# The last expert block of a mixture-of-experts layer: its rows reach their tokens by a product with a gate matrix instead of through memory

## The chip, the cores and the metric

One core of a Trainium2 chip runs the whole program. The metric is the device time of one execution in microseconds (us). A profiled execution is one further run with the hardware profiler on; it has its own time, and a span from its first to its last instruction.

## The reference

The program computes two layers of a small image network on x of shape (4, 384, 32, 32): four images of 1024 tokens with 384 channels. The first layer is attention with relative-position tables and a feed-forward net; the second is a sum of depthwise convolutions and a mixture of four experts. The change concerns only the last part, the experts (S = 1024 tokens of each of B = 4 images, top 2 of 4 experts, hidden size 1536):

```python
def _L1_ffn_ref(x, gate_w, gate_b, w1, b1, w2, b2):
    ...
    topk_vals, topk_idx = jax.lax.top_k(probs, TOP_K)
    mask = jnp.sum(jax.nn.one_hot(topk_idx, NUM_EXPERTS, dtype=probs.dtype), axis=-2)
    masked = probs * mask
    masked = masked / (jnp.sum(masked, axis=-1, keepdims=True) + 1e-09)
    h = jax.nn.gelu(jnp.einsum('bsd,edh->ebsh', x, w1) + b1[:, None, None, :], approximate=False)
    y = jnp.einsum('ebsh,ehd->ebsd', h, w2) + b2[:, None, None, :]
    out = jnp.einsum('bse,ebsd->bsd', masked, y)
    return out
...
t = t + _L1_ffn_ref(_ln_t(t), L1_ffn_gate_w, L1_ffn_gate_b, L1_ffn_w1, L1_ffn_b1, L1_ffn_w2, L1_ffn_b2)
```

A token's output is thus its input plus the outputs of its two experts, each times a gate. All data is float32.

## The kernel before

The kernel computes only the two chosen experts of each token. Tokens are sorted by expert into a buffer in device memory, xs_d, and the experts work through it in **blocks** of 128 rows. As four experts may each leave a block partly filled, there are ALL = 67 blocks. They are cut into four groups, one for each image that becomes ready; the last group has 22 (k = 0 to 21). Results go block by block into y_d, also in device memory, and each token picks its two rows out of it.

`blocks(g, more)` runs a group. `fetch` gathers a block's 128 token rows (xg) with an indirect DMA issued on GpSimd (POOL). `weights` gathers half an expert's weights (w, 2.5 MB) in the same way, `turn` transposes the rows on TensorE (PE) into xT. Then come twelve steps ff: three products into e_ps, a gelu on ScalarE (ACT) into eh, and two steps later, in `second`, the product y_ps. After the last of these VectorE (DVE) adds the bias into yo, and SyncE (SP) writes yo to y_d. So a block's yo is made when PE is already two steps into the next block; only the last block has none behind it.

`more(g, k)` is called after each step and lets other work take its turn in the program's order: the layers ahead, and in the last group from block NOT_LAST = 6 on, `combine(range(B - 1))`. Up to that block all rows of images 0 to 2 are in y_d. `result_rows` computes on DVE the row numbers (row, and as integers pos) of every token of an image. Then twelve times, for 256 tokens at once, `results` gathers four times 128 rows out of y_d on POOL (the tile rows, 16 buffers, always two steps ahead), `weigh` scales the first of each pair on ACT and adds the scaled second on DVE, and `finish` transposes the sums on PE into out_ps, adds them on DVE to the tokens, and lets SP write them out. Tiles out_ps have the PSUM tag m, which has two buffers; e_ps has the tag h (three buffers) and y_ps the tag y (two).

For the last image, image 3, the same is done after all blocks, with `combine([B - 1])`: 16 gathers, all issued ahead of its first `weigh`, and four times `weigh` and `finish`. Its tokens are still on chip, in the tile xb. The source of these gathers is all of y_d:

```python
y_rows = y_d if end else y_d[: (groups[-1]["start"] + NOT_LAST) * BLK]
...
for _ in groups[-1]["combined"]:
    pass
for _ in combine([B - 1]):
    pass
```

The order of instructions on each engine is made by a scheduler from the program's order and the data dependencies between tiles, unless an instruction is wrapped in `pin`, which keeps it in program order. Waits follow from the same dependencies. Every engine then executes its own list in order.

The tile img holds the zero-padded image (128 partitions x 3 x 38 x 38) that the convolutions of an image read. After the convolution of image 3 nothing uses it.

Of the kernel before, what the change touches and what calls it, by code (L numbers as in the profile page):

```python
# [11 lines left out]
F32 = mybir.dt.float32  # L12
AF = mybir.ActivationFunctionType
# [38 lines left out]

NOT_LAST = (2 * (B - 1) * N + NEXP * (BLK - 1)) // BLK - sum(COUNTS[:-1])
MAXB = B * N // BLK
OUTSIDE = 1e6


# [779 lines left out]
def result_rows(nc, small, image, pieces):  # L837


    shape = list(image["mask"].shape)  # L840

    def new(shape, name):
        return small.tile(shape, F32, tag=f"p_{name}", name=f"p_{name}", bufs=1)

    pos, part, step = new(shape, "pos"), new(shape, "prod"), new([P, 1, NEXP], "step")
    nc.vector.tensor_tensor(pos, image["rank"], bcast(pieces[0][1].unsqueeze(1), 1, shape[1]), ALU.add)
    for (_, off0), (lo, off) in zip(pieces, pieces[1:]):
        nc.vector.tensor_tensor(step[:, 0, :], off, off0, ALU.subtract)
        nc.vector.tensor_tensor(part, image["rank"], bcast(lo.unsqueeze(1), 1, shape[1]), ALU.is_ge)
        nc.vector.tensor_tensor(part, part, bcast(step, 1, shape[1]), ALU.mult)  # L850
        nc.vector.tensor_tensor(pos, pos, part, ALU.add)
    row = new([P, shape[1], 2], "fpos")
    for i, pick in enumerate(chosen(nc, new, image["mask"])):
        nc.vector.tensor_tensor(part, pick, pos, ALU.mult)
        nc.vector.tensor_reduce(row[:, :, i : i + 1], part, AX.X, ALU.add)
    nc.vector.tensor_copy(image["pos"], row)


def block_list(nc, small, cst, group, parts, done):
# [76 lines left out]
def rest_phase(tc, cst, x, ao_d, ins, xs_d, y_d, x2_d, out):  # L936
# [9 lines left out]
    with ExitStack() as es:  # L946
# [344 lines left out]
        def blocks(g, more):  # L1291

            xT, xgs = {}, {}

            def fetch(k):
                xg = ld.tile([P, C], F32, tag="xg", name="xg")
                load = nc.gpsimd.indirect_dma_start(
                    xg, None, from_xs, bass.IndirectOffsetOnAxis(ap=g["slot"][:, k, :], axis=0),
                    bounds_check=NEXP * CAP - 1, oob_is_err=False,
                )  # L1300
                for other in g["after"]:
                    after(load, other)
                xgs[k] = xg

            def turn(k):
                xg = xgs.pop(k)
                t = work.tile([P, KC, BLK], F32, tag="xT", name="xT")
                ps = ps_y.tile([P, KC, BLK], F32, tag="t", name="xT_ps")
                for c in range(KC):
                    nc.tensor.transpose(ps[:, c, :], xg[:, c * P : (c + 1) * P], ident)  # L1310
                nc.scalar.copy(t, ps)  # L1311
                xT[k] = t

            def weights(k, fh):
                w = wts[(g["start"] + k) % 2][fh]
                nc.gpsimd.indirect_dma_start(  # L1316
                    w, None, ins["w12"], bass.IndirectOffsetOnAxis(ap=g["row"][:, k, fh : fh + 1], axis=0),
                    bounds_check=NEXP * 2 * P - 1, oob_is_err=False,
                )
                return w  # L1320

            pend = []

            def second(k, ff, hs, w, py):
                o = WB + ff % FH * C
                nc.tensor.matmul(py, hs, w[:, o : o + C], start=(ff == 0), stop=(ff == NF - 1))  # L1326
                if ff == NF - 1:
                    yo = hid.tile([P, C], F32, tag="yo", name="yo", bufs=2)
                    nc.vector.tensor_tensor(yo, py, w[:, WB + FH * C :], ALU.add)  # L1329
                    n = (g["start"] + k) * BLK  # L1330
                    nc.sync.dma_start(y_d[n : n + BLK, :], yo)


            fetch(0)
            ws = {h: weights(*divmod(h, 2)) for h in range(3)}
            turn(0)
            for k in range(g["nb"]):
                py = ps_y.tile([P, C], F32, tag="y", name="y_ps", bufs=2)
                for ff in range(NF):
                    fh, f = divmod(ff, FH)  # L1340
                    h = 2 * k + fh
                    w = ws[h]
                    if ff == 0 and k + 1 < g["nb"]:
                        fetch(k + 1)
                    ph = ps_h.tile([P, BLK], F32, tag="h", name="e_ps")
                    for c in range(KC):
                        o = c * FH * P + f * P
                        nc.tensor.matmul(ph, w[:, o : o + P], xT[k][:, c, :], start=(c == 0), stop=(c == KC - 1))  # L1348
                    hs = hid.tile([P, BLK], F32, tag="eh", name="eh")
                    o = KC * FH * P + f  # L1350
                    nc.scalar.activation(hs, ph, AF.Gelu, bias=w[:, o : o + 1])  # L1351
                    pend.append((k, ff, hs, w, py))
                    if len(pend) > 2:
                        second(*pend.pop(0))
                    if f == 2 and h + 3 < 2 * g["nb"]:
                        ws[h + 3] = weights(*divmod(h + 3, 2))
                    if ff == NF // 2 and k + 1 < g["nb"]:
                        turn(k + 1)
                    more(k)
            for p in pend:  # L1360
                second(*p)

        def combine(bs):


            w = 2 * P
            end = bs[-1] == B - 1
            y_rows = y_d if end else y_d[: (groups[-1]["start"] + NOT_LAST) * BLK]
            pieces = [p for g in groups for p in g["pieces"]]

            def finish(b, n0, xr, zs):
                for c0, c1 in ((0, 2), (2, 3)):
# [7 lines left out]
            def results(b, n0):  # L1380

                zs = []
                for j in range(2):
                    ys = [new_row() for _ in range(2)]
                    for i, y in enumerate(ys):
                        index = images[b]["pos"][:, n0 // P + j, i : i + 1]
                        nc.gpsimd.indirect_dma_start(y, None, y_rows, bass.IndirectOffsetOnAxis(ap=index, axis=0))
                    zs.append(ys)
                if end:
                    return zs, xbs[b][:, :, n0 : n0 + w]  # L1390
                t0 = b * N + n0
                xr = ld.tile([P, KC, w], F32, tag="xr", name="xr")
                nc.sync.dma_start(xr, x2_d[:, t0 : t0 + w].rearrange("(k p) n -> p k n", p=P))
                return zs, xr

            def weigh(b, n0, zs):
                for j, (z, y) in enumerate(zs):
                    gate = images[b]["gate"][:, n0 // P + j, :]
                    nc.scalar.activation(z, z, AF.Copy, scale=gate[:, 0:1])
                    nc.vector.scalar_tensor_tensor(z, y, gate[:, 1:2], z, ALU.mult, ALU.add)  # L1400
                return [z for z, _ in zs]

            if not end:
                for b in (*bs, B - 1):
                    result_rows(nc, small, images[b], pieces)
                    yield 3.0, 0.0
            todo = [(b, n0) for b in bs for n0 in range(0, N, w)]
            ahead = {}
            for i, (b, n0) in enumerate(todo):
                for more in todo[i : i + (len(todo) if end else 2)]:  # L1410
                    if more not in ahead:
                        ahead[more] = results(*more)
                zs, xr = ahead[b, n0]
                for _ in range(0 if end else 5):
                    yield 0.3, 0.0
                zs = weigh(b, n0, zs)
                for _ in range(0 if end else 5):
                    yield 0.3, 0.1
                finish(b, n0, xr, zs)

        xbs, marks = {}, {}

# [91 lines left out]
        def spend(steps):  # L1514
            cost = next(steps, None)
            if cost:
                clock[0] += cost[0]
                clock[1] += cost[1]
            return cost

        def more(g, k):
            clock[0] += 0.05
            clock[1] += 1.36
            if g is groups[-1] and k == NOT_LAST and "combined" not in g:
                g["combined"] = combine(range(B - 1))
            spend(g.get("combined", iter(())))
            while clock[0] < clock[1] and spend(todo):
                pass

        for i, g in enumerate(groups):  # L1530
            blocks(g, lambda k: more(g, k))
            if i + 1 < len(groups):
                while "after" not in groups[i + 1]:
                    next(todo)
        for _ in groups[-1]["combined"]:
            pass
        for _ in combine([B - 1]):
            pass


# [108 lines left out]
```

## Time and profile before

| | |
|---|---|
| three runs | 3029.85, 3033.38, 3039.24 us (median 3033.38) |
| profiled execution | 3047.33 us, span 3045.6 us |
| mean granted PE clock | 0.981 of full speed |
| PE busy | 2916.2 us, 96% of the span |
| DVE busy | 1958.9 us, 64% |
| ACT busy | 1371.9 us, 45% |
| POOL busy | 1158.8 us, 38% |
| gathers rows<-y_d, all 64 | 957 ns each on POOL (median) |
| the last 16 of them | the first at 3016.6, the last at 3036.0 us |

A share of the span says how much an engine works over the whole program, which has several stages with different limits. For the end of the program the chain of waits is the view to read: it goes back from the last instruction to what released it, step by step. Lines in the views name the line of the kernel's text, the engine, and the tile that is written and those that are read (out<-in), without buffer numbers.

### The profile page before, as it was taken

Reading aid. Unit: us, or ns where it says so; the run is one execution under the profiler, and the core shown is the slowest. Engines: PE = TensorE matmul, PEld = TensorE weight load, DVE = VectorE, ACT = ScalarE, POOL = GpSimd, SP = SyncE. Lnnn points to the kernel's source line nnn. Section 1 sums busy time; section 2 is a strip of 40 time slices with the busy share of each in tenths; the row PEclk is TensorE's granted clock in tenths of the full one; section 3 lists DMA queues with packets and bytes.
Section 4 is the critical chain, followed back from the end, with each engine's and each line's share of the span. In section 5 each row is a group of like instructions: output and inputs, shape, how many; then the busy total and the mean of one; then the engine's idle time right before and its main releaser. Section 6 shows DMA issues by size and latency. Waiting matters only on the chain.

```text
span 3045.6 us, 63467 instructions
## 1 busy us (share of the span) xinstructions
PE 2916.2 (96%) x25391; PEld 2018.2 (66%) x25391; DVE 1958.9 (64%) x3577; ACT 1371.9 (45%) x2833; POOL 1158.8 (38%) x1121
## 2 busy tenths in 40 slices
PE   9999999999999999999899889999999999999996
PEld 4556777677777777777533347776577877777775
DVE  3237787777787877787478879999899640001101
ACT  1116766666767676666312332433342243233332
POOL 1115555565656474737300213251124232124412
PEclk9999999999999999999999889999999999999998
DMA  4447667666676766765400405724243055356742
GB/s 156 140 150 218 156 215 161 212 162 217 160 226 155 219 166 206 174 206 155 168 21 35 145 16 192 280 105 153 96 167 126 26 224 228 132 227 252 275 178 73
DMA packets 291720, 500.56 MB, mean 164 GB/s; under 512 B 135632, under 2 KB 221520, under 8 KB 283744
## 3 DMA queue, kind: packets, MB, share of 16 engines
q1 hardware_dynamic: 201760, 269.93, 28.9%
q0 software_dynamic: 37520, 201.63, 17.9%
q10 hardware_dynamic: 52144, 24.94, 4.0%
q8 instruction: 200, 3.28, 0.5%
q14 instruction: 96, 0.79, 0.1%
HBM read 543.58 MB, written 152.37 MB: 229 GB/s over the span
## 4 chain that ended last, share of the span: by engine, by line
PE 74%; DVE 14%; issue 4%; DMA 3%; ACT 2%; POOL 2%; SPq 0%; another core or an unknown queue 0%; POOLq 0%; DVEq 0%; ACTq 0%
PE e_ps L1348 13%; PE y_ps L1326 13%; DVE xb L1136 8%; PE t_ps L430 7%; PE sc_ps L249 7%; PE av_ps L249 7%; PE tabq_ps L249 6%; PE qk_ps L211 4%; PE a_ps L440 3%; PE v_ps L174 2%; PE tv_ps L249 2%; PE proj_ps L1024 2%; DMA s<-sd 1%; PE tap_ps L1184 1%; DVE extra L422 1%
## 5 line engine op out<-in xcount | busy, mean ns | idle before, releaser
L1348 PEld LDWEIGHTS e_ps<-xT,w 128*128 128x128 f32 x4824 | 654.7, 192 | 216.3 <-issue 11.7
L373 POOL TENSOR_TENSOR bias<-b,s 128x416 f32<-128x416 f32 (+24 forms) x656 | 660.7, 1044 | 185.4 <-DMA s<-sd 169.0
L1348 PE MATMUL e_ps<-xT,w 128*128 128x128 f32 x4824 | 668.9, 276 | 13.2 <-ACT xT L1311 5.7
L1326 PE MATMUL y_ps<-w,eh 128*128 128x384 f32 x1608 | 650.8, 490 | 13.1 <-ACT eh L1351 12.7
L1136 DVE SCALAR_TENSOR_TENSOR xb<-img,pack,xb 128x1024 f32<-128x1024 f32 (+1 forms) x539 | 634.5, 1242 | 0.0
L1351 ACT ACTIVATE eh<-e_ps,w 128x128 f32<-128x128 f32 x804 | 293.6, 367 | 717.4 <-PE e_ps L1348 650.6
L1316 POOL DMA_INDIRECT w<-in_w,row x134 | 174.8, 1305 | 731.9 <-PE y_ps L1326 302.7
L422 DVE TENSOR_REDUCE extra<-arow 128x32 f32<-128x32 f32 (+24 forms) x768 | 380.0, 550 | 9.0 <-ACT arow L411 5.5
L401 DVE CUSTOM_DVE_ANT_0 arow<-sc_ps,bias 128x1024 f32<-128x1024 f32 x256 | 311.7, 1218 | 104.8 <-issue 52.0
L411 ACT ACTIVATE arow<-arow,nm 128x1024 f32<-128x1024 f32 x256 | 302.2, 1180 | 68.6 <-DVE nm L401 59.3
L430 PEld LDWEIGHTS t_ps<-ident,arow 128*128 128x128 f32 x2048 | 219.8, 141 | 169.1 <-ACT aT L431 100.6
L431 ACT COPY aT<-t_ps 128x512 f32<-128x512 f32 x512 | 278.6, 604 | 92.2 <-PE t_ps L430 90.3
L430 PE MATMUL t_ps<-ident,arow 128*128 128x128 f32 x2048 | 281.3, 280 | 12.1 <-ACT arow L411 12.1
L1329 DVE TENSOR_TENSOR yo<-y_ps,w 128x384 f32<-128x384 f32 x67 | 37.1, 554 | 392.0 <-PE y_ps L1326 387.2
L249 PE MATMUL sc_ps<-kk,qs 48*32 48x512 f32 x4096 | 276.4, 602 | 6.9 <-DVE nm L401 5.7
L1326 PEld LDWEIGHTS y_ps<-w,eh 128*128 128x128 f32 x1608 | 248.2, 193 | 26.8 <-ACT eh L1351 15.7
L249 PEld LDWEIGHTS av_ps<-aT,vb 128*64 128x64 f32 x4096 | 222.3, 137 | 51.8 <-ACT aT L431 40.0
L338 DVE STREAM_TRANSPOSE b<-tabk_ps 128x480 f32<-128x480 f32 x256 | 218.7, 983 | 35.9 <-PE tabk_ps L249 35.9
L249 PE MATMUL av_ps<-aT,vb 128*64 128x128 f32 x4096 | 237.7, 274 | 0.4 <-ACT aT L431 0.4
L249 PE MATMUL tabq_ps<-tab,kq 48*128 48x480 f32 x512 | 219.5, 578 | 5.7 <-ACT st L342 3.5
L249 PE MATMUL tabk_ps<-tab,kq 48*128 48x480 f32 x512 | 222.6, 581 | 0.0
L249 PEld LDWEIGHTS tabq_ps<-tab,kq 48*128 48x128 f32 x512 | 148.5, 295 | 45.5 <-ACT aT L431 5.6
(212 smaller groups left out, 3136.3 us busy)
## 6 DMA issues: line engine op xcount, KB each, us to landing
sd<-st SPq DMA_DIRECT2D x128, 480.0 KB
s<-sd SPq DMA_DIRECT2D x256, 240.0 KB
xs_d<-arow SPq DMA_DIRECT2D x64, 384.0 KB
tvw<-in_tv SPq DMA_DIRECT2D x120, 192.0 KB
y_d<-yo SPq DMA_DIRECT2D x67, 192.0 KB
qk_d<-vb POOLq DMA_DIRECT2D x48, 256.0 KB
qs<-qk_d SPq DMA_DIRECT2D x256, 48.0 KB
kq<-qk_d ACTq DMA_DIRECT2D x56, 192.0 KB
```

The source lines that it names most:

```text
L249: ins = nc.tensor.matmul(*args, **kw)
L338: turn = nc.vector.transpose(b2.rearrange("p e y x -> p x (e y)")[:, i + j], ps[:, j, : SPAN * IMG])
L373: nc.gpsimd.tensor_tensor(bias[:, y0:y1, :], bass.AP(b2.tensor, b2.offset + (e * IMG + y0) * IMG, [list(b2.ap[0]), [(step * IMG + 1) * IMG ...
L401: nc.vector.tensor_tensor_reduce(s["flat"], ps.rearrange("p h n -> p (h n)"), s["bias"].rearrange("p y x -> p (y x)"), -SCALE, BIG, ALU.ad ...
L411: nc.scalar.activation(s["flat"], s["flat"], AF.Exp, bias=s["nm"], scale=-1.0, accum_out=dn[:, y % YT : y % YT + 1])
L422: pin(nc.vector.tensor_reduce(ex[:, i, :], a[:, p0:p1, :].rearrange("p y x -> p x y"), AX.X, ALU.add))
L430: pin(nc.tensor.transpose(pt[:, j, :], s["flat"][:, k0 : k0 + P], ident))
L431: pin(nc.scalar.copy(aT[:, 4 * g : 4 * g + 4, s["y"] % YB, :], pt))
L1136: ins_ = nc.vector.scalar_tensor_tensor(acc[:, k, y0:y1], img[:, k, dy + y0 : dy + y1, dx : dx + IMG], w7[:, k, dy, dx : dx + 1], acc[:, k ...
L1326: nc.tensor.matmul(py, hs, w[:, o : o + C], start=(ff == 0), stop=(ff == NF - 1))
L1348: nc.tensor.matmul(ph, w[:, o : o + P], xT[k][:, c, :], start=(c == 0), stop=(c == KC - 1))
L1351: nc.scalar.activation(hs, ph, AF.Gelu, bias=w[:, o : o + 1])
```

## The change

1. The last block's result (rows LAST = 66 x 128 and up of y_d) is no longer written to y_d. It stays on chip in yo.
2. `choose` builds a matrix on chip, picked, of 128 x 1024: entry (r, t) is the gate with which row r of the last block counts for token t of image 3, or zero. For each 128 tokens DVE compares the tokens' row numbers, less LAST, with a line 0 to 127 and multiplies with the gates (twice, for the two experts), adds the two, PE transposes, and ACT copies into picked. It advances by one piece with each step of `combine(range(B - 1))`.
3. picked, the line and the working tiles of `choose` lie in the memory of img.
4. The 16 gathers of image 3 read y_d[:LAST] with a bounds check. Rows beyond it aren't fetched, and their gates are set to zero in the tile e_kept. The gathers are put into the program at the first call of `more` after the next-to-last block's yo, which is in the last block.
5. After the blocks come `weigh`, as before but pinned in program order, and `close` in place of `finish`: out_ps is the product of yo and picked plus the sums times the identity matrix, all added up in PSUM. It uses one PSUM tile of each of the tags m, h and y, and DVE adds each of the three to the tokens.

```diff
+        kept = small.tile([P, nj, 2], F32, tag="e_kept", name="e_kept", bufs=1)
+        room = img.rearrange("p k y x -> p (k y x)")
+        picked, line = room[:, :N], room[:, N : N + P]
+
+        def choose(row):
+            gate = images[B - 1]["gate"]
+            rel = small.tile([P, nj, 2], F32, tag="e_rel", name="e_rel", bufs=1)
+            nc.vector.tensor_scalar_add(rel, row, -float(LAST))
+            nc.vector.tensor_scalar(kept, rel, 0.0, None, ALU.is_lt)
+            nc.vector.tensor_tensor(kept, kept, gate, ALU.mult)
+            for n0 in range(0, P, MAXB):
+                nc.vector.tensor_scalar_add(line[:, n0 : n0 + MAXB], pc["blocks"], float(n0))
+            yield
+            last = None
+            for j in range(nj + 1):
+                if last is not None:
+                    ps = ps_m.tile([P, P], F32, tag="m", name="pick_ps")
+                    nc.tensor.transpose(ps, last, ident)
+                    nc.scalar.copy(picked[:, (j - 1) * P : j * P], ps)
+                if j < nj:
+                    hits = [room[:, N + (1 + j % 2 * 2 + i) * P :][:, :P] for i in range(2)]
+                    for i, hit in enumerate(hits):
+                        nc.vector.tensor_scalar(
+                            hit, line, rel[:, j, i : i + 1], gate[:, j, i : i + 1], ALU.is_equal, ALU.mult
+                        )
+                    last, other = hits
+                    nc.vector.tensor_tensor(last, last, other, ALU.add)
+                yield
...
-            y_rows = y_d if end else y_d[: (groups[-1]["start"] + NOT_LAST) * BLK]
+            y_rows = y_d[:LAST] if end else y_d[: (groups[-1]["start"] + NOT_LAST) * BLK]
...
+            def close(b, n0, xr, zs):
+                yo = groups[-1]["result"][1]
+                sums = []
+                for c, (pool, tag) in enumerate(((ps_m, "m"), (ps_h, "h"), (ps_y, "y"))):
+                    ps = pool.tile([P, TOK], F32, tag=tag, name="out_ps", **({"bufs": 2} if tag == "y" else {}))
+                    nc.tensor.matmul(
+                        ps[:, :w], yo[:, c * P : (c + 1) * P], picked[:, n0 : n0 + w], start=True, stop=False
+                    )
+                    sums.append(ps)
+                for j in range(2):
+                    for c, ps in enumerate(sums):
+                        nc.tensor.matmul(
+                            ps[:, j * P : (j + 1) * P], zs[j][:, c * P : (c + 1) * P], ident,
+                            start=False, stop=(j == 1),
+                        )
+                for c, ps in enumerate(sums):
+                    nc.vector.tensor_tensor(xr[:, c, :], xr[:, c, :], ps[:, :w], ALU.add)
+                nc.sync.dma_start(out[b, :, n0 : n0 + w].rearrange("(k p) n -> p k n", p=P), xr)
...
-                        nc.gpsimd.indirect_dma_start(y, None, y_rows, bass.IndirectOffsetOnAxis(ap=index, axis=0))
+                        bound = {"bounds_check": LAST - 1, "oob_is_err": False} if end else {}
+                        nc.gpsimd.indirect_dma_start(
+                            y, None, y_rows, bass.IndirectOffsetOnAxis(ap=index, axis=0), **bound
+                        )
...
+                if end and not i:
+                    yield 0.0, 0.0
+                elif not end:
+                    next(chooser, None)
...
+            if g is groups[-1] and g.get("result", (0,))[0] == g["nb"] - 2 and "tail" not in g:
+                for _ in g["combined"]:
+                    pass
+                g["tail"] = combine([B - 1])
+                next(g["tail"])
...
-        for _ in groups[-1]["combined"]:
-            pass
-        for _ in combine([B - 1]):
+        for _ in groups[-1]["tail"]:
             pass
```

More of the change, by code (lines that the diff above doesn't have):

```diff
@@ L54 @@
 MAXB = B * N // BLK
+LAST = (ALL - 1) * BLK
 OUTSIDE = 1e6
@@ L856, in result_rows @@
     nc.vector.tensor_copy(image["pos"], row)
+    return row
 def block_list(nc, small, cst, group, parts, done):
@@ L1330, in second @@
                     n = (g["start"] + k) * BLK
-                    nc.sync.dma_start(y_d[n : n + BLK, :], yo)
+                    g["result"] = k, yo
+                    if n < LAST:
+                        nc.sync.dma_start(y_d[n : n + BLK, :], yo)
             fetch(0)
@@ L1397, in weigh @@
                 for j, (z, y) in enumerate(zs):
-                    gate = images[b]["gate"][:, n0 // P + j, :]
-                    nc.scalar.activation(z, z, AF.Copy, scale=gate[:, 0:1])
-                    nc.vector.scalar_tensor_tensor(z, y, gate[:, 1:2], z, ALU.mult, ALU.add)
+                    gate = (kept if end else images[b]["gate"])[:, n0 // P + j, :]
+                    keep = pin if end else lambda ins_: ins_
+                    keep(nc.scalar.activation(z, z, AF.Copy, scale=gate[:, 0:1]))
+                    keep(nc.vector.scalar_tensor_tensor(z, y, gate[:, 1:2], z, ALU.mult, ALU.add))
                 return [z for z, _ in zs]
@@ L1404, in combine @@
                 for b in (*bs, B - 1):
-                    result_rows(nc, small, images[b], pieces)
+                    row = result_rows(nc, small, images[b], pieces)
                     yield 3.0, 0.0
+                chooser = choose(row)
             todo = [(b, n0) for b in bs for n0 in range(0, N, w)]
@@ L1418, in combine @@
                     yield 0.3, 0.1
-                finish(b, n0, xr, zs)
+                (close if end else finish)(b, n0, xr, zs)
         xbs, marks = {}, {}
```

## The prediction

> **What bounds the kernel now.** The page's first view gives TensorE (PE) 96% of the span, but a share is an average; the change touches only the end, so I read the end. First, the chain of waits for the last 35 us (start, length, what):
>
> ```profile
> 3011.94 1.96 PE y_ps L1326 x6
> ...
> 3013.92 0.57 DVE yo L1329
> ...
> 3014.51 1.84 DMA y_d<-yo
> ...
> 3016.61 0.97 POOL rows L1387
> ...
> 3032.22 0.96 POOL rows L1387
> ...
> 3033.48 4.08 DMA rows<-y_d,pos
> ...
> 3039.28 0.63 DVE rows L1400
> ...
> 3039.95 0.92 PE out_ps L1376 x3
> ...
> 3040.89 0.69 DVE xb L1377
> ```
>
> The last block's product ends at 3013.9, its rows (yo) are ready at 3014.48, and the span ends at 3045.6: **31.1 us of tail** in which one engine follows another. Its body is POOL's run of 16 gathers, each 0.96 us plus 0.30 us of issue. The waits of that window say what the first gather stood for, and the table by stretches (columns: PE, PEld, DVE, ACT, POOL busy; PE clock; DMA share; GB/s) says what was free meanwhile:
>
> ```profile
> POOL rows L1387 <- DMA y_d<-yo: 31.1, 1, 31.1
> ```
>
> ```profile
> 2935.00:2999.50 64.50, 64.50 (x393) 50.47 (x392) 1.70 (x4) 19.56 (x52) 9.03 (x9) 1.00 0.39 142
> 2999.50:3014.50 15.00, 14.38 (x84) 10.82 (x82) 1.09 (x2) 3.67 (x10) 0.00 (x0) 1.00 0.04 15
> 3014.50:3045.60 31.10, 7.56 (x24) 4.24 (x24) 8.75 (x16) 4.92 (x8) 15.79 (x16) 0.56 0.52 158
> ```
>
> During the whole last block (2999.5 to 3014.5) POOL does nothing and the DMA engines move 15 GB/s; the gathers sat behind one write, of rows that only the last block makes. The timeline has the block before it and the first and last gather:
>
> ```profile
> 2999.48 0.56 DVE L1329 TENSOR_TENSOR yo<-y_ps,w 128x384 f32<-128x384 f32 x1 [15.74 <-PE y_ps L1326]
> ...
> 3016.61 0.97 POOL L1387 DMA_INDIRECT rows<-y_d,pos  x1 [31.11 <-DMA y_d<-yo]
> ...
> 3036.01 0.96 POOL L1387 DMA_INDIRECT rows<-y_d,pos  x1 [0.30 <-issue]
> ```
>
> So the next-to-last block's rows are ready at 3000.04, 14.4 us before the last block's.
>
> **What the Trainium skill says.** "DMA: Bandwidth & Descriptors", section "SWDGE vs HWDGE vs iDMA": GpSimd builds the descriptors of its DMAs in software. The trace agrees: 16 gathers in a row keep POOL at one per 1.26 us. The same page, "Anatomy of one DMA — SWDGE (gpsimd) path", puts about 2.0 us of fixed cost into a DMA, mostly the receipt of the write. The y_d write landed in 1.84 us; a gather's rows were usable 3.07 us after POOL began on it (3016.61 to 3019.68), its 0.96 us on POOL included. "TensorE: Matmul & The Clock Gate", section "What's actually happening": PE falls to half clock after an idle window of about 3.4 us. The trace: last product 3013.9, clock 1.00 until about 3017, 0.50 from 3018 to the end.
>
> **The change, part by part.** The sum is made against the profiled execution (3047.33 us, span 3045.6); the median of the runs shown is 3033.38, 13.95 below it, and I carry the difference over unchanged.
>
> *1. Gathers start a block earlier.* They read y_d without the last block's rows, so the write that they wait for follows 3000.04. From yo's end to the first gather took 3014.48 to 3016.61, 2.13 us; so it starts at 3002.17. In the compiled order POOL has the same instructions in the same order: after the last weight load (2984.50) come the 16 gathers, nothing is queued behind them, and the last block needs none of POOL. Nothing else is moved past.
>
> *2. Their pace.* They now check bounds. The rows that do so (xg 1.01, w 1.00 us) cost 0.045 us more than those that don't (0.957), so one per 1.262 + 0.045 = 1.31 us; 15 steps = 19.6, the last starts at 3021.8. Landing 3.07 to 4.08 us after a start (the chain's 3033.48 piece is the worst); DMA is quiet at first, I take 3.3: **3025.1**.
>
> *3. Work after the last gather.* Before: scaled sum 0.62 (to 3039.90), 2.0 us of transposes and additions to 3041.91, then 3.7 us until the last output has landed. After: the same 0.62; three products with the identity (three e_ps products take 0.67 in the chain, so 0.22 each) of which only the first, with 0.2 us of latency, is ahead of VectorE (DVE); then three additions of 128x256 at 0.414 = 1.24. That is 1.7; 1.95 at half clock; I take 1.8. End: 3025.1 + 0.62 + 1.8 + 3.7 = 3031.2.
>
> *4. What the new products cost.* Per 256 tokens, three products of yo with the gate matrix (y_ps: 0.645 us for 384 columns, so 0.43 each, 1.3) and six with the identity (1.3) in place of six transposes (0.66): 2.6 us of PE at full clock, against 5.2 us for four gathers. The y_d write of the last block (1.84 and 0.26 us of the chain) is gone. ScalarE (ACT) and DVE hold the last image's scalings behind the last block's own instructions, in order, so nothing is weighed before 3012.4 (ACT) and 3014.5 (DVE). By 3014.9 eight gathers have landed; DVE takes per 256 tokens 2 x 0.62 + 3 x 0.414 + about 0.5 of waiting for PE, 3.05 us. Three of four steps end at 3023.7, and the last scaled sum waits for 3025.1. So DVE hides behind the gathers with about 0.8 us to spare.
>
> *5. Building the gate matrix.* 31 small DVE instructions (3 on 16 columns, 4 on 32, 24 on 128), 8 transposes on PE, 8 copies on ACT, beside the combining of images 0 to 2 (2734 to 2935). DVE is busy 32.2 of those 201 us; no row has its shape, but 128x256 costs 0.414, so 24 cost under 10 us and fit. The copies cost at most a gelu of the same size (0.37): 3 us beside 65 of 201, cover the same. PE has no cover: it is busy 190 of 201. A transpose is a sixth of the out_ps group's 0.66: 8 x 0.11 = **0.9 us**. They also share the two PSUM buffers of tag m with out_ps, so a transpose waits until DVE has added the result before it (0.69 us); the compiled order puts three e_ps products (0.67) or a y_ps (0.65) between, so I allow 0.5 us in all, from 0 to 4 (every one waits 0.5). The four writes of the line 0..127 are early, in image 3's block list, hundreds of us ahead of use: nothing.
>
> Everything shifts by 1.4, so the span ends at 3032.6, **13.0 us less**: 3034.3 for a profiled execution, 3020.4 for the median.
>
> **Rivals.**
>
> *PE becomes the end.* If PE is at half clock from 3014.5, a step costs it 5.2 us, four cost 21 and the end is at 3014.5 + 21 + 1 + 3.7 + 1.4 = 3041.6: 4 us less, 3029. For: it was at half clock for this work before. Against: then it had idled 3.9 us; now yo's products follow after 0.6 us, and the first two steps' rows are there. It decides once PE is idle for 3.4 us between 3014 and 3020.
>
> *The gathers don't start early* (a wait still ties them to the block's end). They would then begin at 3014.5, 2.1 us earlier than now but 0.7 slower, and with 1.4 of building the end moves by nothing worth reading: 3032.5. For: one write held all 16 before. Against: the source holds no row of the last block, and they are issued before its last product.
>
> *Slower: the eight transposes stall PE.* Each stands in PE's order ahead of y_ps; behind it wait gelu, the weight load (released by y_ps, and on POOL ahead of gathers and xg), and then the next block. It costs more than the tail gains when each waits over 1.6 us, and shows as slower by 0.3% (9.1 us, about what a measurement of this kernel can tell from no change) from 2.8 us each; with 3.3 us, 26 in all, 3046. For: POOL's queue already delays blocks there (from one y_d write to the next it takes 20.3 us at 2876, 16.1 undisturbed). Against: DVE does the additions within a microsecond of the transposes in nearly all 12 steps, and what a transpose reads is made a whole step ahead.
>
> **How the numbers follow.** Likeliest (0.77): 3020.4; its bounds are -0.9 to +3.5 for the stalls, -0.3 to +0.8 for landing, and the three runs shown differ by 9.4. PE as the end 0.09, at 3029; gathers not early 0.08, at 3032.5; transposes stalling 0.06, at 3046. The range 3014 to 3028 leaves the last three out and little of the first. Faster by over 0.3% (below 3024.3): 0.74 of the first and some of the second, 0.77; within it 0.17; slower 0.06.
>
> **What would show it.** Right: the first tail gather between 3002 and 3005, inside the last block, POOL's 16 gathers ended near 3023 to 3025, 16 to 19 us from the last block's yo to the end, and DVE's last scaled sum waiting for a gather, not for PE. Wrong: the first gather released by a y_d write after the last block; a clock of 0.50 right after it and DVE waiting for out_ps; over 4 us of PE waits for DVE between 2734 and 2935; the last block longer than 14.4 us from yo to yo, which would mean that the gathers disturb it.

## The result, and the profile after

The changed kernel takes **3025.5 us** (median of 22 runs) where the kernel before, run beside it, takes 3035.7 (22 runs, one of them far outside at 10229). The ratio of the two is 0.9961, 95% interval [0.9953, 0.9970]: 11.8 us less, between 9.1 and 14.3 (the two medians differ by 10.2). The prediction had 13.0 us less. That is this comparison; which chip it ran on is not recorded. On the three chips of the experiments, where the kernel before takes 3053 to 3054.5 us, the same change brought nothing that could be measured (ratios 0.9997, 0.9995, 0.9996). Both facts need explaining.

First the profile after: its profiled execution took 3032.55 us, span 3030.8. The table by stretches (length; busy time of PE, PEld, DVE, ACT, POOL with counts; PE clock; DMA share; GB/s), cut at the last two yo: combining stage, last block, tail.

```profile
2740.40:2998.12 257.72, 254.28 (x1568) 200.85 (x1567) 39.74 (x79) 86.62 (x227) 90.86 (x91) 1.00 0.59 212
2998.12:3012.57 14.45, 14.41 (x84) 10.85 (x82) 0.56 (x2) 5.20 (x14) 8.81 (x9) 1.00 0.41 115
3012.57:3030.80 18.23, 11.34 (x72) 9.99 (x72) 9.28 (x21) 2.96 (x5) 7.40 (x8) 0.98 0.57 176
```

In the middle row POOL, idle in the last block before, now works 8.81 us there, and the block still takes 14.45 us from yo to yo. From the last yo's start to the end it is 18.23 us; the same cut through the trace before gives 31.68. The timeline of POOL shows the first gather and the last two:

```profile
3001.33 1.00 POOL L1443 DMA_INDIRECT rows<-y_d,pos  x1 [17.19 <-DMA y_d<-yo]
...
3019.78 1.01 POOL L1443 DMA_INDIRECT rows<-y_d,pos  x1 [0.30 <-issue]
3021.09 1.01 POOL L1443 DMA_INDIRECT rows<-y_d,pos  x1 [0.30 <-issue]
```

The chain of waits ends in a gather's landing (the fifteenth), as predicted, and 2.9 us of ACT, DVE and PE follow it, to the last addition's end at 3027.04:

```profile
3019.78 4.31 DMA rows<-y_d,pos
...
3024.11 0.62 ACT rows L1458
...
3024.76 0.63 DVE rows L1459
...
3025.43 0.50 PE out_ps L1418 x2
...
3025.96 0.75 DVE xb L1423 x2
```

The two profiled executions differ by 14.8 us, more than the kernels do: 13.4 from the next-to-last yo to the end (46.1 against 32.7), and 1.4 in what lies ahead. There the combining stage is 8.2 us shorter after (257.7 against 265.9) and its start 6.9 us later; the first of these matters below. In the trace before, one block of the combining stage (yo at 2733.57 and 2754.12) took 20.55 us; the same block took 16.12 after. The chain of waits **before** has the reason:

```profile
2745.41 0.37 ACT eh L1351
2745.78 4.47 another core or an unknown queue
...
2750.33 0.38 ACT eh L1351
```

A gelu waited for 4.47 us, and the profile found no releaser. It had been there to read when the prediction was made. How typical it is of the kernel before can't be said: this profiled execution (3047.33 us) is slower than 21 of the 22 runs, whose median is 3035.7. The measured 11.8 us are near the 13.4 of the end alone.

### The profile page after: what moved, and what is told of

It is laid out like the page before. It is cut to its first block, busy times and chain, and to the rows that moved or that the text cites. A ratio compares the mean times of both kernels' runs of the same rounds, so it can differ in the third digit from the quotient of the medians.

```text
span 3030.8 us, 63622 instructions
## 1 busy us (share of the span) xinstructions
PE 2928.8 (97%) x25447; PEld 2026.3 (67%) x25447; DVE 1967.2 (65%) x3612; ACT 1374.4 (45%) x2841; POOL 1154.3 (38%) x1121
## 4 chain that ended last, share of the span: by engine, by line
PE 77%; DVE 13%; issue 4%; DMA 3%; ACT 2%; POOL 1%; SPq 0%; POOLq 0%; DVEq 0%; ACTq 0%
PE e_ps L1352 13%; PE y_ps L1328 13%; DVE xb L1138 8%; PE t_ps L431 8%; PE sc_ps L250 7%; PE av_ps L250 7%; PE tabq_ps L250 6%; PE qk_ps L212 4%; PE a_ps L441 4%; PE v_ps L175 2%; PE tv_ps L250 2%; PE proj_ps L1026 1%; PE f_ps L1061 1%; PE tap_ps L1186 1%; PE o_ps L1065 1%
## 5 line engine op out<-in xcount | busy, mean ns | idle before, releaser
L431 PE MATMUL t_ps<-ident,arow 128*128 128x128 f32 x2048 | 283.6, 282 | 14.4 <-ACT arow L412 14.4
```

What stands on the lines that cost most here:

```text
L431: pin(nc.tensor.transpose(pt[:, j, :], s["flat"][:, k0 : k0 + P], ident))
```

## The experiments

All are timed beside the kernel before on the same chip; e11 has one execution. "Last block" is yo to yo, undisturbed 14.44 us; "finish" is from the next-to-last yo's start to the end of the span, 46.1 us in the trace before and 32.7 in the trace after.

| | ratio to before, 95% | median us | last block | finish |
|---|---|---|---|---|
| e1_place | 0.9997 [0.9985, 1.0009] | 3052.6 | 21.79 | 40.8 |
| e2_wait | 1.0017 [1.0007, 1.0027] | 3059.1 | 14.44 | 48.7 |
| e3_nobuild | 0.9990 [0.9981, 1.0000] | 3051.6 | 23.96 | 43.2 |
| e4_best | 0.9996 [0.9984, 1.0008] | 3053.9 | 26.12 | 44.3 |
| e5_same | 0.9995 [0.9985, 1.0005] | 3052.5 | 22.51 | 41.9 |
| e6_pace | 0.9977 [0.9966, 0.9988] | 3045.7 | 14.44 | 40.1 |
| e7_spread | 0.9979 [0.9970, 0.9987] | 3046.3 | 24.67 | 43.9 |
| e8_split | 0.9968 [0.9958, 0.9977] | 3043.0 | 14.44 | 36.7 |
| e9_best | 0.9959 [0.9944, 0.9974] | 3040.0 | 14.44 | 37.7 |
| e10_fours | 0.9962 [0.9947, 0.9977] | 3040.3 | 17.71 | 37.9 |
| e11_noout | one execution | 3037.8 | 14.44 | 36.9 |
| e12_same | 0.9996 [0.9985, 1.0006] | 3052.3 | 23.92 | 42.4 |

e1 to e4 ran on one chip (before: 3054.0 us), e5 to e8 on a second (3054.5), e9 to e12 on a third (3053.3).

### e1_place: the gathers stand at the program's end

```diff
-            if g is groups[-1] and g.get("result", (0,))[0] == g["nb"] - 2 and "tail" not in g:
-                ...
-        for _ in groups[-1]["tail"]:
+        for _ in groups[-1]["combined"]:
+            pass
+        for _ in combine([B - 1]):
```

> Edit: the 16 gathers of image 3 are put into the program after all blocks, as in the kernel before; everything else is as in the changed kernel. Theory (the gathers start early because their source holds no row of the last block; where the program puts them plays no part, since nothing else is on POOL there): the first gather 2.6 us after the next-to-last block's yo and a tail of 17.7 us from the last block's yo to the end, as in the changed kernel, so 0.996 of the kernel before. Rival (the place in the program starts them): the first gather after the last block's yo, a tail of about 29 us, 0.999 to 1.000 of the kernel before.

The compiled order of every engine came out as in the changed kernel, so e1 is that kernel once more: the scheduler puts the gathers beside the block whether the program does or not, and what frees them is their source alone. Yet this copy gained nothing, and its last block took 21.79 us.

### e2_wait: the gathers wait for the last block again

```diff
-                    if n < LAST:
-                        nc.sync.dma_start(y_d[n : n + BLK, :], yo)
+                    nc.sync.dma_start(y_d[n : n + BLK, :], yo)
...
-            y_rows = y_d[:LAST] if end else y_d[: (groups[-1]["start"] + NOT_LAST) * BLK]
+            y_rows = y_d if end else y_d[: (groups[-1]["start"] + NOT_LAST) * BLK]
```

with e1's order of the program.

> Edit: gate matrix and products as in the changed kernel, but the last block's rows are written to y_d again and the gathers' source is all of y_d, so that they wait for that write. Theory (the wait alone is the gain): first gather 2.1 to 2.7 us after the last block's yo, 16 at 1.31 us, landing 3.3 to 4.3, then 0.6 + 1.7 + 3.7: a tail of 31 to 33 us against 31.1 before, and with 1.4 us of building 1.0003 to 1.0011 of the kernel before. Rival (part of the gain comes from the products, or from better packing of the tail): a tail under 28 us.

POOL's wait was back at 31.1 us for a y_d write, the last block was undisturbed, and the finish was 48.7. The new products without the early gathers lose: 1.0017, more than the 1.0003 to 1.0011 that was expected, with 34.2 us from the last yo to the end where the trace before has 31.7. Against e1 the early start is worth 0.0020, 6 us, where the undisturbed finish of the profile after (32.7) would make it 16; 7.35 us of that went into e1's last block.

### e3_nobuild: no gate matrix

```diff
-            for n0 in range(0, P, MAXB):
-                nc.vector.tensor_scalar_add(line[:, n0 : n0 + MAXB], pc["blocks"], float(n0))
             yield
+            return
```

> Edit: the gate matrix is not built (no comparisons, no transposes, no copies; the products read what lies in the image's memory, so the last block's contribution to image 3 is left out of the result). Theory (8 transposes at 0.11 us on PE and up to 0.5 us of waits): 1.4 us faster than the changed kernel, 0.9956 of the kernel before where the changed one has 0.9961; in the profile the 14 blocks of the combining stage shorter by 1 to 2 us, the tail unchanged at 17.7. Rival (the building disturbs the blocks, through DVE or the PSUM buffers): 4 us or more faster, 0.9948 or less.

Inconclusive: 0.9990 against e1's 0.9997, and the intervals overlap. The traces say more on this cost (below).

### e4_best: no bounds check, last output in three pieces

```diff
+        nc.vector.tensor_scalar(image["pos"], row, float(most), None, ALU.min)
...
-                        bound = {"bounds_check": LAST - 1, "oob_is_err": False} if end else {}
+                        bound = {}
...
+                    if n0 + w == N:
+                        nc.sync.dma_start(out[b, c * P : (c + 1) * P, n0 : n0 + w], xr[:, c, :])
```

> Edit: image 3's row numbers are clamped to LAST - 1 on DVE, in the instruction that turns them into integers, so that the gathers need no bounds check; and the last 256 tokens are written out in three pieces, each right after its addition. Theory (the tail is the gather run plus fixed work after it): a gather each 1.26 instead of 1.31 us, 0.7 us less by the last; the last write is 128 KB in place of 384 KB and lands 0.5 to 1.2 us sooner: a tail of 16.0 us against 17.7, 0.9955 of the kernel before. Rival (PE or DVE holds the tail, not the gathers): only the write's share, a tail of 16.7 or more. Second rival (three short writes cost more than one): 17.7 or more.

Each gather took 0.953 us on POOL in place of 1.006, and the span ended 3.0 us after the last output piece was issued instead of 3.7, so both savings exist; the last block took 26.12 us and buried them. Without early gathers (e2) it took 14.44: something in the gathers disturbs it.

### e5_same and e12_same: the changed kernel itself, on two more chips

> This is the changed kernel itself, once more, beside three others. In its first profile the last block took 14.45 us from yo to yo; in the profile of e1, whose instructions are the same in every queue, it took 21.8. Theory A, the disturbance depends on the chip or the execution: where the kernel before takes some 3054 us, the last block takes 20 to 26 us, the combining stage shows its stop of 3 to 5 us near 2745 us, and the ratio is 0.998 to 1.001; on a chip on which the kernel before takes some 3035 us, 14.4 us and a ratio of 0.995 to 0.997. Theory B, it depends on where the program's instructions lie in memory: 14.4 us and a ratio of 0.995 to 0.997 on any chip.

> The changed kernel itself beside e9 and e10. On a chip where the kernel before takes some 3054 us: 0.998 to 1.001, as e1 and e5, with the last block at 20 to 26 us. On one where it takes some 3035 us: 0.995 to 0.997 and 14.4 us; e9 and e10 would then gain less over it, 0 to 0.001.

Theory A: 22.51 and 23.92 us with the very same program that took 14.45. The table by stretches of e12:

```profile
2737.40:3010.55 273.15, 259.88 (x1568) 204.79 (x1567) 39.76 (x80) 85.84 (x227) 90.84 (x91) 0.98 0.56 200
3010.55:3034.47 23.92, 15.67 (x84) 10.89 (x82) 0.55 (x1) 7.31 (x17) 16.10 (x16) 0.87 0.47 130
3034.47:3052.90 18.43, 12.63 (x72) 11.09 (x72) 9.12 (x21) 0.61 (x1) 0.00 (x0) 0.87 0.28 96
```

Against the table after, the tail is the same (18.4 and 18.2); the last block is 9.5 us longer with the same 84 products, and the combining stage 15.4 us longer with the same 1568. The timeline of e5's last block shows how (ACT's gelus eh should come every 1.31 us):

```profile
3009.78 0.37 ACT L1355 ACTIVATE eh<-e_ps,w 128x128 f32<-128x128 f32 x1 [0.95 <-PE e_ps L1352]
...
3011.59 0.37 ACT L1355 ACTIVATE eh<-e_ps,w 128x128 f32<-128x128 f32 x1 [1.44 <-PE e_ps L1352]
...
3012.80 0.83 PE L1352 MATMUL e_ps<-xT,w 128*128 128x128 f32 x6
...
3015.89 0.37 ACT L1355 ACTIVATE eh<-e_ps,w 128x128 f32<-128x128 f32 x1 [3.93 <-remote]
...
3016.31 0.91 PE L1328 MATMUL y_ps<-w,eh 128*128 128x384 f32 x2 [2.04 <-ACT eh L1355]
...
3018.76 0.37 ACT L1355 ACTIVATE eh<-e_ps,w 128x128 f32<-128x128 f32 x1 [2.50 <-PE y_ps L1328]
...
3023.67 0.56 DVE L1331 TENSOR_TENSOR yo<-y_ps,w 128x384 f32<-128x384 f32 x1 [21.95 <-remote]
```

PE's last products into e_ps are issued at 3012.80; the gelu that reads them starts at 3018.76. Two things stand out. Only what PE hands to ACT and DVE is late: PE follows ACT's gelu of 3015.89 within 0.1 us. And the first late gelu comes 7.2 us after the first gather here (3004.36), 7.3 in e1 and 7.3 in e12, while POOL is at the sixth. The word "remote" on a program of one core only says that the profile knows no releaser near by. The trace has the signals themselves: the semaphore of PE that these two gelus wait for goes up at 3015.80 and 3018.68, 0.1 us ahead of each, so ACT is not slow to start. Nor did the clock begin it: PE's clock is 1.00 until 3019.3 and 0.50 from there to the end of the block. It follows, and adds to the delay.

### e6_pace: POOL clears a tile ahead of each gather

```diff
+                        keep = pin if end else lambda ins_: ins_
+                        if end:
+                            pin(nc.gpsimd.memset(y, 0.0))
-                        nc.gpsimd.indirect_dma_start(
+                        keep(nc.gpsimd.indirect_dma_start(
```

> Ahead of each of the last 16 gathers POOL clears the tile that the gather fills (128 rows of 384), some 0.45 us each by the clearings in the trace, so the gathers come every 1.76 us and not every 1.31. Undisturbed, that costs 15 x 0.45 = 7 us: from the next-to-last yo to the end 39.3 us, where the changed kernel's undisturbed profile has 32.7 and the disturbed ones 41 to 44. Theory 1, an unbroken run of more than six gathers at 1.31 us holds up what PE hands to ACT and DVE: the last block is back at 14.4 to 16 us from yo to yo, and the whole takes 39 to 41 us, a ratio to the kernel before that is 0.001 to 0.002 better than e5's if that is disturbed, and 0.002 worse if it is not. Theory 2, any gathers beside the block do it: the last block takes 20 to 27 us, and the end comes 43 us or more after the next-to-last yo, 0 to 0.001 worse than e5.

Theory 1. The gathers came every 1.76 us, and the last block took 14.44. Slower gathers made the kernel faster than e5, by 0.0018, so it isn't gathers beside a block as such. The test is a narrow one, though: the block was over with the seventh gather. If the sixth gather did it at any pace, the gelu due 0.45 us after the sixth's start (at 3019.74) and the yo in the seventh should have been late, as in e5; they were on time.

### e7_spread: the combining stage begins with two fours

```diff
+                        if not end and more == todo[1]:
+                            for _ in range(6):
+                                yield 0.3, 0.0
```

> The combining stage's first eight gathers are issued as two fours with the loads of weights and rows of a block between them, instead of eight in a row; the tail is as in the changed kernel. Theory 1 (an unbroken run does it): the stop of 3 to 5 us near 2745 to 2755 us and the half clock after it are gone, and the kernel is 3 to 7 us faster than e5 where e5 shows the stop (0.998 against 1.000), equal to it where e5 does not. Theory 2 (the stop has nothing to do with the run of gathers): it stays at its place with 3 to 5 us, and the ratio is e5's within 0.001.

Before the change and after it, the combining stage opens with eight gathers in a row. Compiled, e7 has four, a weight load (w), four, and the rows of a block (xg): as many DMAs in a row as before, where w and xg came last, with one break of 0.43 us. The wait without a releaser in that place (3.9 us in e5) is gone, and a stop of 1.2 us ("issue" on PE) remains, 10.9 us after the first gather. But the delay itself is still there. Three gelus in a row (2754.17, 2757.06, 2759.92), the first of them 8.7 us after the first gather, came 2.9 us apart in place of 1.3. Their block took 19.91 us from yo to yo, against 20.30 in e5 and 16.12 in the profile after:

```profile
2742.21 0.56 DVE L1331 TENSOR_TENSOR yo<-y_ps,w 128x384 f32<-128x384 f32 x1 [15.55 <-PE y_ps L1328]
...
2762.12 0.55 DVE L1331 TENSOR_TENSOR yo<-y_ps,w 128x384 f32<-128x384 f32 x1
```

What is shorter lies later: the stage's second block took 16.11 us where e5 has 19.14, the ninth 17.74 where e5 has 20.51; some others are longer, by up to 1.3 us. The medians fell by 6.2 us against e5. That the order in this stage matters is shown by this. That it ended the disturbance is not so, and whether the break or the place of w gained the time is open. In its tail, left as it was, the last block took 24.67 us, and its first late gelu (3018.29, by 0.4 us) came while POOL was at the fifth gather.

### e8_split: six gathers beside the block, ten behind it

```diff
-                    nc.vector.tensor_tensor(yo, py, w[:, WB + FH * C :], ALU.add)
+                    g["last"] = nc.vector.tensor_tensor(yo, py, w[:, WB + FH * C :], ALU.add)
...
+                        if end and n0 // P * 2 + j * 2 + i >= 6:
+                            after(load, groups[-1]["last"])
```

with e1's order of the program.

> Six of the last 16 gathers run beside the last block, the other ten wait for its yo. Theory 1 (disturbance only after six or more in a row): the last block takes 14.4 us, the tenth of the others starts 2.65 + 9 x 1.31 = 14.4 us after that yo's end, and the end comes 14.45 + 0.56 + 14.4 + 1.0 + 8.7 = 39.1 us after the next-to-last yo, against 32.7 undisturbed and 41 to 44 disturbed: 0.001 better than a disturbed e5. Theory 2 (any gathers beside the block): the last block takes 17 us or more, and the end comes at 42 us or more.

Theory 1 again, and a better finish than expected, 36.7 us. The waits of its end have:

```profile
POOL rows L1443 <- DVE yo L1331: 4.5, 1, 4.5
```

A planned wait of 4.5 us on POOL takes the place of the 7.4 to 9.5 us that the block lost in e1, e5 and e12. The timeline has one gelu late by 0.57 us after the sixth gather (3017.92 after 3016.04), then the next two catch up: the disturbance begins at the sixth and, as far as this run tells, needs more gathers to go on.

### e9_best and e10_fours: e7 and e8 together, and another form of the second

e9 is e7 and e8 together. e10 is e7 with one clearing ahead of every fifth, ninth and thirteenth tail gather:

```diff
+                        if end and n0 + j + i and not (j or i):
+                            pin(nc.gpsimd.memset(y, 0.0))
```

> e7 and e8 together: the combining stage's first eight gathers in two fours, six tail gathers beside the last block and ten behind its yo. Theory 1 (unbroken runs of gathers hold up PE's results): the two gains add, 0.9979 and 0.9968 less the 0.9995 of the changed kernel itself make 0.995 to 0.996 where the kernel before takes some 3054 us; the last block takes 14.4 us, the end comes 36.6 us after the next-to-last yo, and the middle has at most 1.2 us of stop. Theory 2 (what e7 gained was chance): 0.997.

> e7, and in the tail POOL clears one tile of 128 rows of 384 (0.43 us, as measured in e6, 0.70 with its gaps) ahead of every fifth, ninth and thirteenth gather alone: runs of four with pauses of 1.0 us. If a pause of that length after four gathers ends the run, the last block takes 14.4 us and the end comes 32.7 + 3 x 0.70 = 34.8 us after the next-to-last yo, the shortest of all: 0.9945 to 0.9955. If it is the gathers' mean pace over some 7 us that counts (here 1.31 + 0.70/4 = 1.49 us, in e6 2.02), the last block is late by 3 us or more, and the end comes at 38 to 42 us: 0.996 to 0.998.

(The 2.02 us for e6 in that text is a slip; it is 1.76.) The gains added up: **0.9959 and 0.9962 where the changed kernel itself, beside them, had 0.9996**; e9 is 12.3 us faster than it by the medians. e9's last block is undisturbed. Its combining stage takes 262.9 us between the same two yo, against 273.2 in e12 and 268.8 in e5:

```profile
2745.70:3008.56 262.86, 254.73 (x1567) 200.83 (x1566) 39.64 (x80) 86.07 (x227) 89.88 (x91) 1.00 0.59 208
3008.56:3023.00 14.44, 14.40 (x84) 10.85 (x82) 0.55 (x1) 5.18 (x13) 6.04 (x6) 1.00 0.34 97
```

Its first block, of 19.90 us, has the late gelus of e7's:

```profile
2757.66 0.37 ACT L1355 ACTIVATE eh<-e_ps,w 128x128 f32<-128x128 f32 x1 [2.51 <-PE e_ps L1352]
2760.55 0.37 ACT L1355 ACTIVATE eh<-e_ps,w 128x128 f32<-128x128 f32 x1 [2.52 <-PE e_ps L1352]
```

e10's pauses turned out short: a clearing hides 0.14 us of issue, and only 0.28 us were added at each, a mean step of 1.37 us. That was not enough. The first late gelu moved from after the sixth gather to the seventh, and the last block took 17.71 us:

```profile
3008.47 0.37 ACT L1355 ACTIVATE eh<-e_ps,w 128x128 f32<-128x128 f32 x1 [0.95 <-PE e_ps L1352]
3010.50 0.37 ACT L1355 ACTIVATE eh<-e_ps,w 128x128 f32<-128x128 f32 x1 [1.66 <-PE e_ps L1352]
3013.38 0.37 ACT L1355 ACTIVATE eh<-e_ps,w 128x128 f32<-128x128 f32 x1 [2.51 <-PE y_ps L1328]
```

So a gap of 0.59 us after every four isn't enough to end the run; the pause of 1.0 us that was planned has not been run.

### e11_noout: e9 without three output writes

```diff
+                if n0 + w == N:
                     nc.sync.dma_start(out[b, :, n0 : n0 + w].rearrange("(k p) n -> p k n", p=P), xr)
```

> e9 without the first three of the last image's four writes of 384 KB to the output (768 of its 1024 tokens are not written). If the writes beside the last gathers make them land later, the last gathers land after 3.1 to 3.3 us, as the early ones do, where e8's last took 4.0, and the end comes about 0.8 us earlier, 35.8 us after the next-to-last yo. If the gathers' own number makes it, it stays at 4.0 and 36.6.

The scalings on ACT in e11 wait for one gather each and show the landing; the gathers behind which they stand were issued at 3017.27, 3019.90, 3022.52 and 3025.14:

```profile
3020.37 0.62 ACT L1461 ACTIVATE rows<-rows,e_kept 128x384 f32<-128x384 f32 x1 [2.05 <-DMA rows<-y_d,pos]
3023.06 0.61 ACT L1461 ACTIVATE rows<-rows,e_kept 128x384 f32<-128x384 f32 x1 [2.07 <-DMA rows<-y_d,pos]
3025.75 0.62 ACT L1461 ACTIVATE rows<-rows,e_kept 128x384 f32<-128x384 f32 x1 [2.07 <-DMA rows<-y_d,pos]
3028.23 0.62 ACT L1461 ACTIVATE rows<-rows,e_kept 128x384 f32<-128x384 f32 x1 [1.86 <-DMA rows<-y_d,pos]
```

That is 3.1 to 3.2 us for each. In e9, with the writes, the same four took 3.6, 3.6, at most 4.9 and 3.9. So the output writes beside the gathers lengthen their landing by 0.5 us and more. What that is worth at the end isn't shown: the finish was 36.9 us where 35.8 was expected, 0.8 us shorter than e9's, but e8, with all its writes, has 36.7.

## Why the prediction was right, and where it was not

**Step 1, the early start: right, 0.5 us mis-sized.** The first gather began at 3001.33, inside the last block, 2.65 us after the yo's end at 2998.68 and not 2.13. POOL's wait for a y_d write fell from 31.1 to 17.2 us. What frees the gathers is the source, as argued; the place in the program played no part (e1), and with the source widened the wait was back (e2).

**Step 2, the pace: right.** 1.32 us per gather, 19.76 for 15 steps against 19.6. The bounds check costs what was taken from other rows, 0.05 us (1.006 against 0.953 in e4). **The landing was mis-sized**: 3.3 us assumed because "DMA is quiet at first", 4.31 measured in the fifteenth. It is quiet at first, but when the last gathers run, the first output quarters are being written (from 3016.8 on), and e11 shows that such writes lengthen the landing. The change itself moved them together. The chain runs through the fifteenth gather and a scaling on ACT (0.62 us) that the sum did not have. As the fifteenth starts 1.31 us ahead of the last, that takes back most of both: from the last gather's start (3021.09) to the scaled sum's end (3025.39) it took 4.30 us, and the sum had 3.3 + 0.62 = 3.92.

**Step 3, after the last gather: right.** From the scaled sum's end (3025.39) to the last addition's (3027.04) 1.65 us against 1.8, then 3.76 against 3.7.

**Step 4, the cover of the new products: right.** DVE's last scaled sum waited for ACT, which waited for a gather, and not for PE. The rival "PE becomes the end" fell with it: the clock in the tail was 0.98. It was 0.85 to 0.87 in the tails of e5 and e12, where it had fallen to 0.50 in the disturbed block.

**Step 5, building: oversized.** It was priced at 1.4 us. Two neighbouring blocks of the combining stage that hold three of the eight transposes took 17.17 and 18.34 us after, from yo to yo, and 17.10 and 18.33 before. First after, then before:

```profile
2823.69 0.56 DVE L1331 TENSOR_TENSOR yo<-y_ps,w 128x384 f32<-128x384 f32 x1 [0.36 <-PE y_ps L1328]
...
2840.86 0.56 DVE L1331 TENSOR_TENSOR yo<-y_ps,w 128x384 f32<-128x384 f32 x1 [6.95 <-PE y_ps L1328]
...
2859.20 0.55 DVE L1331 TENSOR_TENSOR yo<-y_ps,w 128x384 f32<-128x384 f32 x1
```

```profile
2822.15 0.55 DVE L1329 TENSOR_TENSOR yo<-y_ps,w 128x384 f32<-128x384 f32 x1
...
2839.25 0.56 DVE L1329 TENSOR_TENSOR yo<-y_ps,w 128x384 f32<-128x384 f32 x1 [6.30 <-PE y_ps L1326]
...
2857.58 0.55 DVE L1329 TENSOR_TENSOR yo<-y_ps,w 128x384 f32<-128x384 f32 x1
```

That is 0.08 us for three, a few tenths for all: the six blocks with seven of the eight took 103.00 us after (from 2774.20) and 102.94 before (from 2772.90). The rival with the stalls of 2.8 us and more on each transpose had no support: the waits of the transposes and their weight loads for DVE between 2740 and 2950 were 0.3 and 1.0 us in all. e3 could not resolve so little.

The sum: from the next-to-last yo's end to the end it had 31.15 us, and 32.12 were measured. That is 0.5 us too little in the start, 0.2 in the pace and 0.4 from the last gather to the scaled sum; about a microsecond too much in the building makes up for it. So the 13.0 is near the traces' own net gain (13.4 less a few tenths), in part because errors cancel; 11.8 [9.1, 14.3] were measured.

**What the prediction did not have** is that the gathers disturb the block that was to cover them. It named the sign (a last block "longer than 14.4 us ... would mean that the gathers disturb it") and gave it no price and no chance. In the first comparison's profiled execution it didn't occur, and nothing in the prediction says why it shouldn't: that this comparison fell where the block was left alone is **luck**. The 20.3 us block at 2876 that the prediction put down to POOL's queue took 17.6 after with POOL's order unchanged, so it may have been a sign of the same kind. In the executions of the same program on three chips (e1, e5, e12) the disturbance took 7.4 to 9.5 us of the 13.4. That leaves some 4 us of gain in the finish (46.1 against 40.8 to 42.4); the measured 0.9 to 1.5 us, about 3 either way, is a little less, and as there is no trace of the kernel before on those chips, the rest stays open.

So does the mechanism. Shown is: on these chips a run of gathers at 1.31 us sets it off (e5 and e12 against e6 and e8), not the number in all; it begins while POOL is at the fifth to the seventh; it holds up what PE hands on; six alone cost nothing, and a step of 1.76 us cost nothing in the seven gathers that the block covered. The runs don't tell whether PE finishes late or its signal comes late, as the ends of products are modelled in the trace; nor whether POOL's own work on a gather does it or the transfer, as both went slower together in e6. Why the first execution escaped it isn't known, and whether the chip or the execution decides isn't either. No run has a gap for each gather of the combining stage.

## What to carry to other kernels

Work that is moved under a busy engine isn't free because other engines do it: ask of the profile before whether the same kind of work has already run beside the same stage, and compare that block's length with its neighbours' (20.55 us against 16.1 here, behind a run of eight gathers). If a run of transfers disturbs its cover, shorten or slow it before giving up the overlap: with six early and ten late the finish was 36.7 us, where the trace before has 46.1. And a gain of 0.4% on one chip is worth repeating on another.

## What the runs showed of the hardware

- A run of indirect gathers, each 1.0 us on POOL and 0.30 us apart, delayed the hand-over from PE to ACT and DVE from about the sixth gather on, on three chips (the last gelu of e5's block by over 5 us), while ACT's hand-over to PE stayed within 0.1 us in that block. In one profiled execution elsewhere the same run delayed nothing. At one per 1.76 us there was none in the seven gathers seen.
- An indirect gather of 128 rows of 1.5 KB landed 3.1 to 3.2 us after its start in e11, without output writes beside it, and after 3.6 to 4.6 beside output writes of 384 KB (e8, e9, the profile after).
- The same program took 3025.5 us in the first comparison and 3052.3 to 3052.6 on the three chips of the experiments; its combining stage took 257.7 us in the first profile and 268.8 to 273.2 in the other three. Those 11 to 15 us are part of the difference; where the rest lies is open.
